# The attention's own values along the rows: four transposes of a broadcast column in place of a product of 512 columns

## The chip, the core and the metric

The kernel runs on one core of a Trainium2 chip. The metric is device time in microseconds (us) of one execution, the median of three runs. Five engines work side by side, each through its own instructions in order: PE (matrix products and transposes, its weight loads shown apart as PEld), DVE (elementwise work and reductions), ACT (activations and copies), POOL (here it issues the gathers) and SP (which issues most plain DMAs).

## The reference, cut to what matters

Sixty-four graphs of 256 nodes with 256 features pass through four layers over one adjacency matrix: two gated layers, an attention layer, a gated layer. The change touches the attention layer alone:

```
feats = jnp.einsum('bni,oi->bno', data, W1)
f1 = jnp.einsum('bno,o->bn', feats, W2) + b2[0]
logits = f1[:, :, None] + f1[:, None, :]
coefs = jax.nn.softmax(jax.nn.leaky_relu(logits) + bias1, axis=-1)
vals = jnp.einsum('bij,bjo->bio', coefs, feats)
return vals + bias2 + data
```

So each node has one number f1, its "own value". The logit of the pair (i, j) is f1 of i plus f1 of j. With nodes i on partitions and j along the row, f1 of i is a column (one number for each partition), and f1 of j has to be laid along the row of every partition. How this row is made is what changes. `bias1` is the adjacency matrix `adj`.

## The kernel before, in words

**Tiling.** Graphs go in pairs. A pair is `st["h"]` (nodes on partitions) and `st["hT"]` (features on partitions, `[128, 2, 2, 256]`: feature half, graph, node). Two streams, side a and side b, take turns over the pairs, so there are 16 rounds with two pairs each and 32 calls of `attention` (L430) in all. Everything is float32.

**Heavy and light work.** `beside` (L904) lays two things next to each other: the edge scores of one side's gated layer (`scores`, L695: tiles `ga` made on PE from `pre` and `pick`, in three PSUM buffers, and tiles `fetched` gathered by POOL's DMAs, both reduced by DVE to `junk` with a sum) and, as light work, what the other side does between its scores (`finish`, the two `turn`s, `attention`, and `before`, which makes the tables of the next layer). A `yield` of the light work says how many tiles of the heavy work are written out at that place; `yield 0` says none. Side a's attention stands beside side b's second gated layer, side b's attention beside side a's last one. At the end of a `beside`, `rm` is made from the scores and `spread` multiplies it on PE.

**Order.** The text of the program gives the order in which instructions are considered. The framework then lays down every engine's order before the run, from its own estimate of times, and lets an instruction that it takes to be ready go ahead of one that it takes to be waiting: the trace has the first `qb` product (L438) starting at 1667.54 us, in the midst of the transposes of `turn`, which are written ahead of it. At run time every engine keeps that order.

**PSUM.** `psum()` hands out one of five buffers, each one bank of 2 KB for each partition; `ga` has three more.

**The fetch.** `before` (L642) makes `pu` and `pv`, writes them to tables in DRAM (DMAs `tableu`, `tablev` from SP's queue), and POOL gathers from them (`fetch`, L807), each gather queued behind the one before it. The last gather of a layer has to land before DVE can finish that layer's scores, and `rm` after them.

**The attention, step by step.** At set-up, L257 makes `w2q`: the weights W1 transposed, with the product of W1 and W2 as column 256. `qb` (L255, L268) is that column repeated 128 times. Then, for each pair:

1. `rows` (L436) gets a product with `qb` as the stationary operand and all 512 columns of the pair, in two steps over the feature halves: every partition then holds f1 of all nodes along the row, without b2.
2. For each graph g and node half m, a product with `w2q` (257 columns) gives `feats` and, in column 256, f1 of the nodes on the partitions. DVE adds twice b2 to that column and puts it into `own` (L445, shown as `own_f` in the profile). ACT copies the 257 columns to `f`.
3. After both halves of a graph, ACT makes `logits` as `rows` plus `own` as its bias, two instructions for each graph.
4. DVE makes `e` from `logits` (leaky ReLU), adds `adj` with a running extreme `top`, and ACT takes the exponential into `e`. PE transposes `e`, and the products with `f` follow.

Of the kernel before, what the change touches and what calls it, by code (L numbers as in the profile page):

```python
# [9 lines left out]
FP = mybir.dt.float32  # L10
I32 = mybir.dt.int32
AF = mybir.ActivationFunctionType
ALU = mybir.AluOpType
AX = mybir.AxisListType

P = 128
B, N, D = 64, 256, 256
# [45 lines left out]
def blk(c):  # L63
    return slice(c * P, (c + 1) * P)
# [37 lines left out]
def adj_seq_kernel(ctx: ExitStack, tc: tile.TileContext, a: dict, out: bass.AP):  # L102
# [15 lines left out]
    tensor, vector, scalar = Noting(nc.tensor), Noting(nc.vector), Noting(nc.scalar)  # L118
    mm = tensor.matmul
# [6 lines left out]
    const = ctx.enter_context(tc.tile_pool(name="const", bufs=1))  # L126
# [3 lines left out]
    ident = const.tile([P, P], FP, name="ident")  # L130
# [13 lines left out]
    def vec(name, c):  # L144
        return vecs[:, VEC[name], c : c + 1]

    def sca(name):
        return scas[:, SCA[name] : SCA[name] + 1]
# [26 lines left out]
    for l in GNN:  # L175
        halfb2[l] = const.tile([P, 1], FP, name=l + "halfb2")
        vector.tensor_scalar(halfb2[l], sca(l + "b2"), 0.5, None, ALU.mult)
    twob2 = const.tile([P, 1], FP, name="twob2")
    vector.tensor_scalar(twob2, sca("L2_gnn_b2"), 2.0, None, ALU.mult)
    ones = const.tile([P, P], FP, name="ones")  # L180
    nc.gpsimd.memset(ones, 1.0)

# [69 lines left out]
    zbrow = const.tile([P, D], FP, name="zbrow")  # L252
    bias2 = const.tile([P, D], FP, name="bias2")
    w2q = const.tile([P, 2, D + 1], FP, name="w2q")
    qb = const.tile([P, 2, P], FP, name="qb")  # L255

    def attention_weights(one, psum):  # L257
        nc.scalar.dma_start(out=bias2, in_=a["L2_gnn_bias2"].partition_broadcast(P))
        nc.sync.dma_start(out=w2q[:, :, 0:D], in_=a["L2_gnn_W1T"].rearrange("(c p) e -> p c e", p=P))
        w2n = one.tile([P, 2, D], FP, tag="aT", name="w2n")  # L260
        nc.sync.dma_start(out=w2n, in_=a["L2_gnn_W1"].rearrange("(c p) e -> p c e", p=P))
        t = psum().rearrange("p a b -> p (a b)")
        for m in range(2):
            for c in range(2):
                mm(out=t[:, m : m + 1], lhsT=w2n[:, c, blk(m)], rhs=vec("L2_gnn_W2", c), start=c == 0, stop=c == 1)
        vector.tensor_copy(w2q[:, :, D], t[:, 0:2])
        for c in range(2):
            vector.tensor_scalar(qb[:, c, :], ones, w2q[:, c, D : D + 1], None, ALU.mult)  # L268

    def last_bias(one):  # L270
        bmrow = one.tile([P, D], FP, tag="hb", name="bmrow")
# [5 lines left out]
    def other_weights(one, psum):  # L277
        for l in GNN:
            z_weights(l)
            if l != GNN[0]:  # L280
                pre_weights(l)
            if l == GNN[1]:
                attention_weights(one, psum)
        last_bias(one)
# [10 lines left out]
    def stages(pools):  # L295
        fm, wk, one, ps, ga = (pools[k] for k in ("fm", "wk", "one", "ps", "ga"))
# [6 lines left out]
        def psum():  # L303
            return ps.tile([P, 2, 256], FP, tag="ps", name="ps")
# [7 lines left out]
        def flip(o, src):  # L312

            for m in range(2):
                for c in range(2):
                    tensor.transpose(o[:, m, blk(c)], src[:, c, blk(m)], ident)

        def hT_tile(st):
            return one.tile([P, 2, 2, N], FP, tag="hT" + st["side"], name="hT")

        def h_tile(st, g):
            return fm.tile([P, 2, D], FP, tag=f"h{g}" + st["side"], name=f"h{g}")
# [107 lines left out]
        def attention(st):  # L430
            hT, f = st["hT"], feats
            e, eT = [], []
            hb = st["h"]
            logits = one.tile([P, 2, 2, N], FP, tag="mT" + st["side"], name="logits")
            own = one.tile([P, 2, 2], FP, tag="own_f", name="own_f")
            rows = psum()  # L436
            for c in range(2):
                mm(out=rows, lhsT=qb[:, c, :], rhs=hT[:, c], start=c == 0, stop=c == 1)  # L438
            for g in range(2):
                e.append(one.tile([P, 2, N], FP, tag=f"e{g}", name=f"e{g}"))  # L440
                for m in range(2):
                    t = psum().rearrange("p a b -> p (a b)")
                    for c in range(2):
                        mm(out=t[:, 0 : D + 1], lhsT=hT[:, c, g, blk(m)], rhs=w2q[:, c, :], start=c == 0, stop=c == 1)
                    vector.tensor_scalar(own[:, g, m : m + 1], t[:, D : D + 1], twob2, None, ALU.add)  # L445
                    scalar.copy(f[g][:, m, 0 : D + 1], t[:, 0 : D + 1])
                    yield 0
                for m in range(2):
                    scalar.activation(
                        logits[:, g, m, :], rows[:, g, :], AF.Identity, bias=own[:, g, m : m + 1]  # L450
                    )
            for g in range(2):

                top = one.tile([P, 2], FP, tag=f"top{g}", name="top")
                vector.scalar_tensor_tensor(e[g], logits[:, g], 0.01, logits[:, g], ALU.mult, ALU.max)
                for m in range(2):
                    vector.tensor_tensor_reduce(
                        out=logits[:, g, m, :], in0=e[g][:, m, :], in1=adj[:, m, :], scale=-1.0, scalar=3.0e38,
                        op0=ALU.add, op1=ALU.min, accum_out=top[:, m : m + 1],
                    )  # L460
                for m in range(2):
                    scalar.activation(
                        e[g][:, m, :], logits[:, g, m, :], AF.Exp, bias=top[:, m : m + 1], scale=-1.0
                    )
                yield 2 - g
            st["h"], st["hT"] = [], hT_tile(st)

            def flip_h(g):
                t = psum()
                flip(t, st["h"][g])  # L470
                scalar.copy(st["hT"][:, :, g, :], t)


            st["flip"] = flip_h
            for g in range(2):
                t = psum()
                flip(t, e[g])
                eT.append(logits[:, g])
                scalar.copy(eT[g], t)
                yield 1  # L480
                h = h_tile(st, g)
                for m in range(2):
                    t = psum().rearrange("p a b -> p (a b)")
                    for c in range(2):
                        mm(out=t[:, 0 : D + 2], lhsT=eT[g][:, c, blk(m)], rhs=f[g][:, c, :], start=c == 0, stop=c == 1)
                    r = one.tile([P, 1], FP, tag="r", name="r")
                    vector.reciprocal(r, t[:, D + 1 : D + 2])
                    vector.scalar_tensor_tensor(h[:, m, :], t[:, 0:D], r, hb[g][:, m, :], ALU.mult, ALU.add)
                    if (g, m) == (1, 0):
                        flip_h(0)  # L490
                    yield 0, 1
                st["h"].append(h)

        return dict(psum=psum, product=product, load=load, mixed=mixed, finish=finish, attention=attention)


# [544 lines left out]
```

## Time and profile before

| what | value |
|---|---|
| median of three runs | 3490.05 us (3488.29 to 3501.34) |
| the profiled execution, its own time | 3499.89 us |
| its span, first to last instruction | 3498.2 us |
| mean granted TensorE clock | 0.993 |
| PE's idle time in all (span less busy) | 107 us |
| `ps<-hT,qb`, the products that are replaced | 128 records, median 592 ns |
| `ps<-w2q,hT` | 512 records, median 379 ns |
| `own_f`, DVE, 128x1 | 128, median 218 ns |
| `f<-ps`, ACT, 128x257 | 128, median 374 ns |
| `logits<-ps,own_f`, ACT, 128x256 | 128, median 479 ns |

How to read it: a float32 product appears as two records for each step over the features (64 products of 512 columns, 128 records), a transpose as one. PE's records overlap, since a product is still running out when the next begins; what a product takes of PE's time is read from the distance between starts, and not from its own length. In a timeline a row is a run of like instructions: its start, its length, the engine, the tiles (out<-in), the shape, how many, and in brackets how long the engine was idle before it and what ended that.

### The profile page before, as it was taken

The numbers are of one execution on the slowest core, as the hardware profiler recorded it, in microseconds if no ns is written. First come the engines' busy times: TensorE is split into PE (matmuls) and PEld (weight loads), VectorE is DVE, ScalarE is ACT, GpSimd is POOL, SyncE is SP. The second block draws the span as 40 slices with busy tenths as digits, with TensorE's granted clock in tenths as the row PEclk, the third lists the DMA queues.
The fourth block names the chain that finished last, engine by engine and source line by source line (L and its number), as shares of the span: only waits on it lengthen the run. The fifth ranks groups of instructions, "written<-read, shape, count | busy, mean of one in ns | idle before, by whom it ended". The sixth has DMA issues, their size and how long they took to land.

```text
span 3498.2 us, 48226 instructions
## 1 busy us (share of the span) xinstructions
PE 3391.1 (97%) x14200; PEld 2079.5 (59%) x14200; DVE 2626.2 (75%) x10526; ACT 1554.0 (44%) x2833; POOL 2409.6 (69%) x1882
## 2 busy tenths in 40 slices
PE   6999999999999999999999999999999999999998
PEld 3566565665656556565665656556565565656655
DVE  5777777777777777777777777777777777777776
ACT  2444444444444444544444444444444444444442
POOL 3767767677776767677677776776767667676765
PEclk7999999999999999999999999999999999999999
DMA  5788787877878878788787878778788788787875
GB/s 146 164 181 187 166 204 163 188 174 172 199 168 193 179 169 191 172 191 176 174 192 165 197 168 184 178 167 198 165 190 176 173 191 171 190 178 175 190 166 125
DMA packets 289070, 620.81 MB, mean 177 GB/s; under 512 B 39072, under 2 KB 56352, under 8 KB 288800
## 3 DMA queue, kind: packets, MB, share of 16 engines
q0 software_dynamic: 204800, 461.49, 66.6%
q1 hardware_dynamic: 82416, 154.96, 12.6%
q8 instruction: 115, 1.88, 0.2%
q10 hardware_dynamic: 1584, 1.20, 0.1%
q14 instruction: 155, 1.27, 0.1%
HBM read 500.06 MB, written 117.44 MB: 177 GB/s over the span
## 4 chain that ended last, share of the span: by engine, by line
PE 62%; POOL 10%; DMA 10%; DVE 8%; issue 7%; ACT 3%; another core or an unknown queue 0%; POOLq 0%; ACTq 0%; SPq 0%; DVEq 0%
PE ps L79 48%; PE ga L79 13%; POOL fetched L820 9%; DMA fetched<-tablev,ids_v 6%; DVE junk L79 3%; DMA fetched<-tableu,ids_u 3%; ACT pre L79 2%; DVE rm L79 1%; POOL left L820 1%; DVE sa L79 1%; DMA tableu<-pu 1%; DVE own L79 1%; ACT val L79 1%; ACT pu L79 1%; DVE mT L79 0%
## 5 line engine op out<-in xcount | busy, mean ns | idle before, releaser
L820 POOL DMA_INDIRECT fetched<-tablev,ids_v x832 | 1313.7, 1579 | 415.3 <-issue 256.1
L820 POOL DMA_INDIRECT fetched<-tableu,ids_u x832 | 840.5, 1010 | 548.8 <-DMA tableu<-pu 285.4
L79 DVE SCALAR_TENSOR_TENSOR junk<-fetched,L_gnn_w2row 128x256 f32<-128x256 f32 x1664 | 642.4, 418 | 205.8 <-DMA fetched<-tablev,ids_v 203.7
L79 PE MATMUL ga<-pre,pick 128*128 128x512 f32 x1408 | 721.5, 607 | 36.0 <-ACT pre L79 24.6
L79 PE MATMUL ps<-L_gnn_w,hT 128*128 128x512 f32 x1536 | 706.7, 597 | 5.8 <-DMA hT<-in_xT_dram 5.8
L79 DVE SCALAR_TENSOR_TENSOR junk<-ga,L_gnn_w2row 128x256 f32<-128x256 f32 x1408 | 537.3, 419 | 110.6 <-PE ga L79 94.6
L79 PEld LDWEIGHTS ps<-L_gnn_w,hT 128*128 128x128 f32 x1536 | 279.7, 190 | 323.2 <-issue 296.3
L79 ACT COPY pre<-pv 64x512 f32<-64x512 f32 x704 | 434.1, 617 | 70.8 <-DVE pv L79 47.3
L79 ACT COPY pre<-pu 64x1024 f32<-64x1024 f32 x352 | 361.4, 1044 | 7.4
L79 PE MATMUL ps<-sa,h 128*128 128x256 f32 x1536 | 359.8, 380 | 4.7 <-DVE sa L79 4.7
L79 PEld LDWEIGHTS ps<-sa,h 128*128 128x128 f32 x1536 | 291.7, 190 | 114.4 <-issue 62.5
L79 PEld LDWEIGHTS ga<-pre,pick 128*128 128x128 f32 x1408 | 248.5, 190 | 183.6 <-issue 92.5
L79 ACT COPY pu<-ps 128x256 f32<-128x256 f32 x384 | 142.8, 372 | 478.2 <-PE ps L79 450.3
L79 ACT ACTIVATE hb<-hT,L_gnn_zbias,scas 128x512 f32<-128x512 f32 x128 | 97.4, 807 | 479.3 <-DVE hT L79 368.1
L79 DVE TENSOR_TENSOR rm<-gva,val 128x256 f32<-128x256 f32 x768 | 279.8, 419 | 28.7 <-ACT val L79 21.2
L79 PE MATMUL ps<-adj,h 128*128 128x256 f32 x1280 | 296.8, 383 | 3.9 <-issue 3.9
L79 PEld LDWEIGHTS ps<-adj,h 128*128 128x128 f32 x1280 | 241.6, 191 | 74.1 <-issue 40.0
L79 DVE TENSOR_TENSOR pv<-ps,L_gnn_b1row 128x256 f32<-128x256 f32 x384 | 161.3, 420 | 135.5 <-ACT pu L79 128.8
L79 PEld LDWEIGHTS ps<-rm,gu 128*64 128x64 f32 x3072 | 174.7, 137 | 144.5 <-issue 54.1
L79 PE MATMUL ps<-rm,gu 128*64 128x128 f32 x3072 | 218.8, 280 | 32.6 <-DVE rm L79 31.0
L79 ACT COPY aT<-ps 128x512 f32<-128x512 f32 x192 | 112.4, 585 | 299.7 <-PE ps L79 267.5
L79 PE MATMUL ps<-mT,L_gnn_Wm 128*128 128x512 f32 x512 | 240.6, 592 | 0.0
(153 smaller groups left out, 4239.6 us busy)
## 6 DMA issues: line engine op xcount, KB each, us to landing
tableu<-pu SPq DMA_DIRECT2D x192, 256.0 KB
tablev<-pv SPq DMA_DIRECT2D x192, 256.0 KB
hT<-in_xT_dram SPq DMA_DIRECT2D x32, 512.0 KB
h<-in_x_dram SPq DMA_DIRECT2D x64, 256.0 KB
out_dram<-h SPq DMA_DIRECT2D x64, 256.0 KB
fetched<-tableu,ids_u POOLq DMA_INDIRECT x832
fetched<-tablev,ids_v POOLq DMA_INDIRECT x832
L_gnn_w<-in_L_gnn_W_dram SPq DMA_DIRECT2D x6, 256.0 KB
```

The source lines that it names most:

```text
L79: self.last = getattr(self.engine, op)(*a, **k)
L820: this = nc.gpsimd.indirect_dma_start(out=to, out_offset=None, in_=rows, in_offset=bass.IndirectOffsetOnAxis(ap=ids, axis=0), compute_op=( ...
```

## The change

The product with `qb` goes, and with it `qb`, `twob2` and `own`. In its place DVE takes column 256 of each `w2q` product, adds b2 and writes it 128 times side by side into the first 128 columns of `e[g][:, m]` (a tile that was there already, and is written anew later in the same call). A new inner function `across(g)` has PE transpose these two 128x128 squares into `rows[:, g]`, which lays f1 plus b2 along the row of every partition, and has ACT make the two `logits` of that graph with column 0 of the square as the bias. `across(0)` is called after the product of the second graph's first half (g, m) = (1, 0), and `across(1)` after the last product. So the logits of graph 0 are written down one product later than before, and PE's transposes read what DVE has written. Both terms now carry b2 once, where before one carried it twice.

```
-            own = one.tile([P, 2, 2], FP, tag="own_f", name="own_f")
             rows = psum()
-            for c in range(2):
-                mm(out=rows, lhsT=qb[:, c, :], rhs=hT[:, c], start=c == 0, stop=c == 1)
+
+            def across(g):
+
+                for m in range(2):
+                    tensor.transpose(rows[:, g, blk(m)], e[g][:, m, 0:P], ident)
+                for m in range(2):
+                    scalar.activation(
+                        logits[:, g, m, :], rows[:, g, :], AF.Identity, bias=e[g][:, m, 0:1]
+                    )
+
             for g in range(2):
                 e.append(one.tile([P, 2, N], FP, tag=f"e{g}", name=f"e{g}"))
                 for m in range(2):
                     t = psum().rearrange("p a b -> p (a b)")
                     for c in range(2):
                         mm(out=t[:, 0 : D + 1], lhsT=hT[:, c, g, blk(m)], rhs=w2q[:, c, :], start=c == 0, stop=c == 1)
-                    vector.tensor_scalar(own[:, g, m : m + 1], t[:, D : D + 1], twob2, None, ALU.add)
+
+                    vector.tensor_scalar(
+                        e[g][:, m, 0:P], t[:, D : D + 1].to_broadcast([P, P]), sca("L2_gnn_b2"), None, ALU.add
+                    )
                     scalar.copy(f[g][:, m, 0 : D + 1], t[:, 0 : D + 1])
                     yield 0
-                for m in range(2):
-                    scalar.activation(
-                        logits[:, g, m, :], rows[:, g, :], AF.Identity, bias=own[:, g, m : m + 1]
-                    )
+                    if (g, m) == (1, 0):
+                        across(0)
+            across(1)
```

At set-up these go as well:

```
-    twob2 = const.tile([P, 1], FP, name="twob2")
-    vector.tensor_scalar(twob2, sca("L2_gnn_b2"), 2.0, None, ALU.mult)
...
-    qb = const.tile([P, 2, P], FP, name="qb")
...
-        for c in range(2):
-            vector.tensor_scalar(qb[:, c, :], ones, w2q[:, c, D : D + 1], None, ALU.mult)
```

## The prediction

> **What bounds the kernel.** I read the page first, then PE's timeline around both kinds of attention, DVE's and ACT's there, and last the chain of waits.
>
> ```profile
> span 3498.2 us, 48226 instructions
> ...
> PE 3391.1 (97%) x14200; PEld 2079.5 (59%) x14200; DVE 2626.2 (75%) x10526; ACT 1554.0 (44%) x2833; POOL 2409.6 (69%) x1882
> ...
> PE 62%; POOL 10%; DMA 10%; DVE 8%; issue 7%; ACT 3%; another core or an unknown queue 0%; POOLq 0%; ACTq 0%; SPq 0%; DVEq 0%
> ```
>
> PE is idle for 107 us only, yet it holds 62% of the chain that ended last: POOL and the gathers' DMAs hold another 20%. Two things run neck and neck, PE's work and the path table, gather, landing, scores, `rm`. What is taken from PE counts where the chain lies on PE.
>
> PE around side b's attention (start, length, then what):
>
> ```profile
> 1709.56 1.07 PE L79 MATMUL ps<-ident,hT 128*128 128x128 f32 x8
> 1710.47 1.88 PE L79 MATMUL ps<-hT,qb 128*128 128x512 f32 x4
> 1712.19 3.64 PE L79 MATMUL ps<-w2q,hT 128*128 128x257 f32 x16
> 1715.66 1.89 PE L79 MATMUL ga<-adj,h 128*128 128x256 f32 x8
> 1717.39 1.02 PE L79 MATMUL ga<-pre,pick 128*128 128x512 f32 x2
> 1718.25 0.60 PE L79 MATMUL ps<-ident,e 128*128 128x128 f32 x4
> ```
>
> No brackets: PE starts each row as the last one lets it. The starts give prices: 1712.19 - 1710.47 = 1.72 us for the product with `qb`; 0.91 us for eight transposes, 0.11 us each; 3.47 us for the four `w2q` products, 0.87 us each. Between them and the transposes of `e` lie two rows of heavy work (1.73 and 0.86 us) that cover the softmax. All 32 calls show these distances: the transposes of `e` begin 6.06 us after the first `w2q` product every time.
>
> DVE and ACT on side a:
>
> ```profile
> 1670.99 0.22 DVE L79 TENSOR_SCALAR own_f<-ps,twob 128x1 f32<-128x1 f32 x1 [0.77 <-PE ps L79]
> 1671.86 0.22 DVE L79 TENSOR_SCALAR own_f<-ps,twob 128x1 f32<-128x1 f32 x1 [0.65 <-PE ps L79]
> ```
>
> ```profile
> 1671.24 0.37 ACT L79 COPY f<-ps 128x257 f32<-128x257 f32 x1 [1.47 <-DVE own_f L79]
> 1671.51 0.48 ACT L79 ACTIVATE logits<-ps,own_f 128x256 f32<-128x256 f32 x1
> 1672.11 0.37 ACT L79 COPY f<-ps 128x257 f32<-128x257 f32 x1
> ```
>
> DVE stands idle for the column and takes it 0.20 us after the product's end. ACT's copy of the same bank starts 0.03 us after DVE's read ends, though neither writes it: accesses of two engines to one bank come one after the other.
>
> **The change part by part.** *PE.* Each call loses 1.72 us and gains four transposes, 4 x 0.11 = 0.43 us (the row of four `ident,e`: 1718.68 - 1718.25 = 0.43 too). Net 1.29 us, 32 calls: 41.3 us of PE work. Their weight loads overlap, as in the rows of transposes that are there.
>
> *DVE.* 128 instructions become 128x128 from a column in PSUM. The trace has no such form. Bounds: `own_f` itself, 218 ns below; the slower of the two `qb<-ones,w2q` (128x128, 557 ns) above. Nearest is this row, of that size and from PSUM:
>
> ```profile
> L79 DVE TENSOR_TENSOR picko<-ps,scratch x2: 280/286/291, 47.9 to 48.1; 128x128 f32<-128x128 f32 x2
> ```
>
> I take 286 ns: 68 ns more, x128 = 9 us of DVE in all (0 to 43). On side a the idle 0.65 to 0.77 us before each `own_f` covers it; without that it costs 68 ns of delay each.
>
> *ACT, SP, POOL.* The same copies and logits; no DMA is added or moved. The set-up loses `twob2` and both `qb`, 0.98 us of DVE in the first 73 us, while other weights load; I count nothing (0 to 1 us gain).
>
> *The new waits.* PE's transposes now wait for DVE; behind them in PE's queue stand the heavy rows. On side a, taking the `qb` time out, `w2q` would start at 1669.92 - 1.72 = 1668.20. DVE is in `h<-ps,bias` until 1670.22, so the first two squares are done at 1670.79 (two times 286 ns); PE finishes the third product at 1668.20 + 2.60 = 1670.80: no stall. `across(1)` needs the fourth square (product done 1671.89, +0.20, +0.29 = 1672.38) and, by the one-after-the-other of a bank, the end of ACT's two reads for graph 0 (from about 1671.2, two times 0.48, so 1672.2). PE is free at 1671.89: 0.5 us, which the 1.73 us of `ga<-adj,h` fills if it is laid ahead.
>
> The Trainium skill's page "PSUM — Partial Sum Buffer" (PSUM bank collisions) says that any two engines on one bank and quadrant must be kept apart, reads too, which speaks against keeping both graphs in one bank as `rows` does; the 0.03 us above agrees, and the sum has that wait either way.
>
> *What is late next.* The transposes of `e`. Before, 2.77 us passed from the end of graph 0's second logits (1672.86) to the last exponential (1675.63). Now: 1672.2 + 2.77 = 1674.97, while PE gets there at 1668.20 + 3.47 + 0.43 + 1.73 + 0.86 = 1674.69. Late by 0.28 us. On side b DVE reaches the squares only behind `h<-ps,bias` (until 1712.69): two squares until 1713.27, transposes, logits to about 1714.7, exponentials to 1717.4, against PE at 1716.96: 0.5 us late, and up to 1.9 if three `hb` of 0.48 us stay ahead of the squares. The heavy row behind the transposes of `e` (0.86 us, in both timelines) can fill such a gap if it is laid ahead; it may or may not be, so I take half: 0.14 us for a, 0.25 for b.
>
> *What of it reaches the end.* I asked for the chain from 2 us before to 16 us after the first `w2q` product of each of the 32 calls. It lies on PE for over half of the stretch in 22 (15 of side a, 7 of side b), and on POOL, DMA and issue in 10 (1 and 9). One of the latter, side b at 1712, ends so:
>
> ```profile
> 1725.45 7.25 DMA fetched<-tablev,ids_v
> ...
> 1732.72 0.78 DVE junk L79 x4
> 1733.50 0.35 DVE pv L79
> ...
> 1737.86 1.12 PE ga L79 x2
> ```
>
> A gather lands, DVE does its scores and only then `pv`, which ACT and PE wait for. PE that comes 1.29 us sooner waits longer there: I count 0 for these ten (0 to 12.9 us). A gather that starts after an earlier gain starts sooner with it, so the 22 keep theirs: 22 x 1.29 = 28.4 us. Less 15 x 0.14 + 7 x 0.25 = 3.9. **Sum: -24.5 us**, from the profiled 3499.9 to 3475. The profiled execution is 9.8 us above the median; from the median it is 3465.5, say **3465**. Bounds of the parts: all 32 gain, nothing late, is -41.3 (3449); the 22 alone, a late by 0.28 and b by 1.9, is 28.4 - 4.2 - 13.3 = -11 (3479).
>
> **The rivals.** *The gathers take the whole over.* With 1.29 us less on PE in each call, more stretches become like 1712, and those that were PE's gain little. For: 20% of the chain is there, and PE waits for `rm` 33 times, 31.0 us. Against: after side a's attention the second half of `spread` starts 1.0 us after its `rm`, after side b's 1.9 us, so that the gain mostly fits in. If a third of it is left, -41.3 / 3 = -14: 3476; if none, 3490.
>
> *Slower: PE stands behind DVE.* Place: `across`, where a square is laid on DVE behind scores whose gather hasn't landed. The trace has DVE waiting for landings 148 times, 203.7 us, 1.4 us each. If both `across` of a call meet one, PE loses 2.8 us and gains 1.29: 32 x 1.5 = +48, 3538. It decides from 1.29 us of stall for each call. For: before, PE needed nothing of DVE for `rows`; now DVE's queue is PE's. Against: in none of the 32 calls were the transposes of `e` moved from their 6.06 us, so no landing got into this stretch.
>
> *The order falls out otherwise.* Engines are laid out anew from changed times over the whole kernel; waits that PE has now, such as 24.6 us for `ACT pre`, may grow or go. Either sign, about half a per cent: 3473 to 3507, taken as no change.
>
> *The clock.* The granted clock is 1.00 in the 2 us around the eight transposes at 1709.56. If transposes lowered it to half for the 3.47 us of `w2q` in each call, that would be 32 x 3.47 = 111 us more: 3576. The Trainium skill's "TensorE: Matmul & The Clock Gate" (Part 4: PE-mode transpose) says that transposes don't count as PE being busy for that clock; the trace, which has runs of eight at 1.00, bears out none of it.
>
> **How the numbers follow.** The forecast has 0.58; the gathers 0.16 (half of it past 0.5% faster); order 0.15; slower 0.09; the clock 0.02. Half a per cent, 17.5 us, is what a measurement of this kernel tells from no change. Faster (below 3472.6): most of the forecast's share, 0.52, half the gathers', 0.08, and 0.04 of the order's: 0.64. Slower (over 3507.5): 0.09 + 0.02 + 0.03 = 0.14. Same: 0.22. The range goes from all 32 gains with some 6 us of the runs' own spread, 3443, to where the slower case begins, 3502.
>
> **What would show it.** `ps<-hT,qb` is gone, 128 more records of transposes with `e` (0.11 us between starts); the new DVE form near 286 ns; the transposes of `e` begin 6.5 us after the first `w2q` product, not 6.06, without a bracket of over 0.5 us; PE's busy time down by 30 to 45 us. Wrong it is if PE's waits for `e` or `ACT logits` sum to over 20 us, if the squares stand behind scores on DVE, or if PE's idle time (107 us) grows by what its work lost.

## The result, and the profile after

The changed kernel takes 3468.32 us (median of 7 runs, 3455.23 to 3472.99) against 3490.05 us. The medians lie 22 us apart. The ratio over all 14 runs (their means are 3465.75 and 3492.72 us) is 0.9923 with a 95% interval of 0.9903 to 0.9943: 27 us faster, 20 to 34. It was forecast at 3465. From here on, 27 us is the gain that the experiments have to account for.

The page of the changed kernel: span, busy time of each engine, the chain by engine.

```profile
span 3466.6 us, 48384 instructions
...
PE 3361.7 (97%) x14200; PEld 2067.6 (60%) x14200; DVE 2639.6 (76%) x10523; ACT 1557.2 (45%) x2833; POOL 2416.1 (70%) x1882
...
PE 68%; POOL 9%; DMA 7%; issue 7%; DVE 6%; ACT 3%; ACTq 0%; POOLq 0%; DVEq 0%
```

PE's busy time fell by 29 us, just short of the 30 to 45 that the prediction named as a sign; its idle time stayed (107 us before, 105 now), and its share of the chain rose from 62 to 68%.

PE around side b's attention:

```profile
1693.57 1.07 PE L79 MATMUL ps<-ident,hT 128*128 128x128 f32 x8
1694.48 2.77 PE L79 MATMUL ps<-w2q,hT 128*128 128x257 f32 x12
1697.09 0.27 PE L79 MATMUL ps<-ident,e 128*128 128x128 f32 x1
1697.20 0.60 PE L79 MATMUL ps<-w2q,hT 128*128 128x257 f32 x2
1697.63 0.27 PE L79 MATMUL ps<-ident,e 128*128 128x128 f32 x1
1697.74 0.60 PE L79 MATMUL ps<-w2q,hT 128*128 128x257 f32 x2
1698.18 1.03 PE L79 MATMUL ga<-adj,h 128*128 128x256 f32 x4
1699.04 0.38 PE L79 MATMUL ps<-ident,e 128*128 128x128 f32 x2
1699.26 1.03 PE L79 MATMUL ga<-adj,h 128*128 128x256 f32 x4
1700.13 1.02 PE L79 MATMUL ga<-pre,pick 128*128 128x512 f32 x2
1700.99 0.81 PE L79 MATMUL ps<-ident,e 128*128 128x128 f32 x4
```

Again no brackets: the four new transposes were laid between products that PE had to do anyway, graph 1's in the midst of `ga<-adj,h`, and PE waits for none of them. From `ident,hT` to the transposes of the exponentials (the last row) it is 7.42 us, where it was 8.69. That last row takes 0.81 us, where it took 0.60: behind the first of the four, the weight load for the others waits for an exponential, which has come late.

```profile
1701.25 0.31 PEld L79 LDWEIGHTS ps<-ident,e 128*128 128x128 f32 x3 [0.26 <-ACT e L79]
```

DVE's new form (least, median and most ns):

```profile
L79 DVE TENSOR_SCALAR e<-ps,scas x128: 334/344/352, 177.3 to 3393.5; 128x128 f32<-128x128 f32 x128
```

Where the gain is and where part of it stays is best read in stretches of PE's row. I took the starts of four kinds of rows in every round and the mean over the rounds: from `ident,hT` to the first transposes of the exponentials; from there to the first product of `before`; on to `spread`; and on to the next attention's `ident,hT`.

| stretch, us | a before | a after | b before | b after |
|---|---|---|---|---|
| turn to exponentials | 8.65 | 7.50 | 8.68 | 7.41 |
| to `before` | 6.94 | 6.80 | 6.80 | 7.01 |
| to `spread` | 10.46 | 10.46 | 13.87 | 13.67 |
| to the next turn | 16.34 | 17.09 | 141.58 | 141.54 |
| all | 42.40 | 41.85 | 170.95 | 169.64 |

In the first two rows, which hold the attention, a gains 1.29 us and b 1.06 (1.27 less the 0.21 of the late exponential): 16 x 2.35 = 38 us. Side a gives 0.75 back in the row "to the next turn". There PE waits for `ACT pre`: 1.0 us in each round before, now up to 2.3. One such place, in the chain of waits of the changed kernel (start, length, what; pieces of `issue` left out):

```profile
398.42 1.55 POOL fetched L824
...
400.28 7.62 DMA fetched<-tablev,ids_v
...
407.92 0.78 DVE junk L79 x4
408.70 0.35 DVE pv L79
...
413.05 1.13 PE ga L79 x2
```

It is the picture that the prediction showed for side b: the last gather lands, DVE does its scores, then `pv`, then ACT's `pre`, and PE's product waits for that.

Of the 12 us that side a gives back in 16 rounds, 8.6 are longer waits. In the rest PE's rows themselves run slower, as here, behind a wait:

```profile
1677.79 2.08 PE L79 MATMUL ga<-pre,pick 128*128 128x512 f32 x2 [2.25 <-ACT pre L79]
1679.80 1.71 PE L79 MATMUL ps<-rm,gu 128*64 128x128 f32 x16
```

In the kernel before, these rows take 1.12 and 1.09 us. The granted clock is 0.50 from 1677.68 to 1681.09 us. Leaving out the first 120 us and the last 40 us, the changed kernel has three such stretches of 3.4 us, each behind a wait of PE of 1.9 to 2.4 us (two for `ACT pre`, one ahead of `ps<-sa,h`); the kernel before has none. Not every wait of that length brings one: behind the 2.33 us at 410.72 the clock stays at 1.00. Half the speed for 10.2 us is 5 us, a part of the difference between the 38 us of the table and the 29 us by which PE's busy time fell.

### The profile page after: what moved, and what is told of

Same layout as the page of the kernel before. It is cut to its first block, busy times and chain, and to the rows that moved or that the text cites. A ratio compares the mean times of both kernels' runs of the same rounds, so it can differ in the third digit from the quotient of the medians.

```text
span 3466.6 us, 48384 instructions
## 1 busy us (share of the span) xinstructions
PE 3361.7 (97%) x14200; PEld 2067.6 (60%) x14200; DVE 2639.6 (76%) x10523; ACT 1557.2 (45%) x2833; POOL 2416.1 (70%) x1882
## 3 DMA queue, kind: packets, MB, share of 16 engines
q14 instruction: 155, 1.27, 0.1%
## 4 chain that ended last, share of the span: by engine, by line
PE 68%; POOL 9%; DMA 7%; issue 7%; DVE 6%; ACT 3%; ACTq 0%; POOLq 0%; DVEq 0%
PE ps L79 52%; PE ga L79 16%; POOL fetched L824 8%; DMA fetched<-tablev,ids_v 4%; DVE junk L79 3%; ACT pre L79 2%; DMA fetched<-tableu,ids_u 2%; DVE rm L79 1%; DMA tableu<-pu 1%; POOL left L824 1%; DVE sa L79 1%; ACT val L79 1%; ACT pu L79 1%; DVE own L79 0%; DVE pv L79 0%
## 5 line engine op out<-in xcount | busy, mean ns | idle before, releaser
L79 PE MATMUL ga<-pre,pick 128*128 128x512 f32 x1408 | 723.5, 609 | 37.0 <-ACT pre L79 27.4
L79 PE MATMUL ps<-rm,gu 128*64 128x128 f32 x3072 | 218.7, 281 | 23.0 <-DVE rm L79 22.6
L79 PE MATMUL ps<-aT,L_gnn_Wa 128*128 128x512 f32 x512 | 240.6, 592 | 0.0
```

The source lines that it names most:

```text
L79: self.last = getattr(self.engine, op)(*a, **k)
```

## The experiments

My theory: PE has 1.29 us less to do in each call, the heavy rows cover the new waits, and the gathers keep some of the gain from the end. Rivals: the gain comes from another order of the engines' instructions; DVE's wider writes count; the missing part is lost in the attention itself. Ratios are to the kernel before, run beside each on the same chip.

### DVE's part alone

```
-                    vector.tensor_scalar(own[:, g, m : m + 1], t[:, D : D + 1], twob2, None, ALU.add)
+                    vector.tensor_scalar(
+                        e[g][:, m, 0:P], t[:, D : D + 1].to_broadcast([P, P]), twob2, None, ALU.add
+                    )
...
-                        logits[:, g, m, :], rows[:, g, :], AF.Identity, bias=own[:, g, m : m + 1]
+                        logits[:, g, m, :], rows[:, g, :], AF.Identity, bias=e[g][:, m, 0:1]
```

> The kernel before, with its product of 512 columns kept, and only DVE's part of the change: the column is written 128 times into e instead of once into own. If the gain comes from PE's work (my theory), nothing of it is here: DVE has 128 x 126 ns = 16 us more (344 ns in the changed kernel against 218), which PE's work covers, so 3480 to 3500 us beside 3490 before. If DVE's work counts in full, 16 us slower, 3506. If the gain comes from another order of the engines' work, which the change of one DVE form can bring as well, some 3470.

Measured: 3562.11 us, ratio 1.0192 (1.0165 to 1.0218), 67 us slower. All three expectations missed it. PE's timeline around side a's attention in this kernel:

```profile
1047.69 1.02 PE L79 MATMUL ga<-pre,pick 128*128 128x512 f32 x2
1048.55 0.60 PE L79 MATMUL ps<-ident,e 128*128 128x128 f32 x4
1048.98 1.88 PE L79 MATMUL ga<-pre,pick 128*128 128x512 f32 x4
1050.70 1.91 PE L79 MATMUL ps<-f,logits 128*128 128x258 f32 x8
1052.45 0.60 PE L79 MATMUL ps<-ident,e 128*128 128x128 f32 x4
1053.78 1.14 PE L79 MATMUL ps<-f,logits 128*128 128x258 f32 x4 [0.73 <-ACT logits L79]
```

Three heavy products (`ga<-pre,pick`, 0.86 us, two records each) are there to cover the softmax. In the kernel before one stands ahead of each pair of transposes' products: one before the first `ident,e`, one behind it, one behind the second. Here two stand behind the first, none behind the second, and PE waits 0.73 us for ACT's copy (the last bracket). One DVE form was changed, and the order laid down ahead of the run put one product elsewhere, and with it rows of DVE and ACT.

These waits sum to 22.9 us. The greater part of the 67 us stands later: side a's stretch "to the next turn" takes 19.25 us, where it took 16.34, which is 47 us in 16 rounds. There PE waits for `ACT pre` (53.3 us in this run, 24.6 before), and the granted clock falls to 0.50 in twelve stretches, 44 us together, each behind a wait of 2.2 to 3.1 us: up to 22 us of the loss.

### Both calls of across at the end

```
-                    if (g, m) == (1, 0):
-                        across(0)
+            across(0)
             across(1)
```

> The changed kernel with both calls of across after the last product. Graph 0's logits are written down one product (0.87 us) later. If the heavy rows cover the softmax, as they did before, PE does the same work in about the same time: 3468 us within 6. If the place of across(0) carries the gain, by starting the softmax of graph 0 early, PE waits for e up to 0.87 us in each call, 28 us: up to 3496.

Measured: 3494.81 us, ratio 0.9996 (0.9982 to 1.001). The whole gain is gone, though PE does the same work. Its timeline on side a:

```profile
1032.23 1.88 PE L79 MATMUL ga<-pre,pick 128*128 128x512 f32 x4
1033.94 0.60 PE L79 MATMUL ps<-ident,e 128*128 128x128 f32 x4
1034.38 1.02 PE L79 MATMUL ga<-pre,pick 128*128 128x512 f32 x2
1035.28 2.01 PE L79 MATMUL ps<-f,logits 128*128 128x258 f32 x8
1037.12 0.60 PE L79 MATMUL ps<-ident,e 128*128 128x128 f32 x4
1038.45 1.14 PE L79 MATMUL ps<-f,logits 128*128 128x258 f32 x4 [0.73 <-ACT logits L79]
```

It waits not for the first exponentials, as I had written, but at the same place as the last kernel in the attention: here two heavy products went ahead of the first transposes, and again none was left behind the second. These are PE's longest waits in this kernel, summed (us in total, times, longest):

```profile
PE ga L79 <- ACT pre L79: 44.5, 32, 2.4
PE ps L79 <- ACT logits L79: 22.6, 31, 0.7
```

The first of the two lines has grown as well (24.6 us in the kernel before, 27.4 in the changed one): side b's stretch "to `spread`" now takes 15.08 us (13.67 in the changed kernel).

### The heavy products held in their place

Both kernels again, with a heavy product of the attention's stretch held behind the transposes that it is written after: `behind` asks that an instruction be issued after the one written last before it on the same engine. (`held` is emptied when `attention` ends.)

```
+            held.append(True)
             for g in range(2):
                 t = psum()
                 flip(t, e[g])
...
-                    with stay(tensor):
+                    with behind(tensor) if held else stay(tensor):
                         mm(out=t, lhsT=pick[:, k, 4 * m + i, :], rhs=pre[:, n], start=True, stop=True)
```

> Both across after the last product, as in the run before (3495 us), and the heavy products of the attention's stretch held behind the transposes of e that they are written after. In that run one of three heavy products (0.86 us) had gone ahead of the first transposes of e, and none was left to cover ACT's copy between the second transposes and their products: PE waited 0.73 us for ACT logits in each call, 22.6 us in all. If that one product's place is the cause, this kernel is back at the changed kernel's time, 3466 to 3478 us (ratio 0.992 to 0.995), with no such wait and at most 0.9 us of wait for e in its stead. If the later logits are the cause, it stays at 3490 to 3500.

Measured: 3468.7 us, ratio 0.9934 (0.9919 to 0.9948). The wait for `ACT logits` is gone and the gain is back with `across(0)` still at the end, so that its place is not what carries the gain. Between the traces of these two kernels 29 us have gone: 9 in the stretches from `ident,hT` to `before`, where the product was put back, and 20 in side b's stretch "to `spread`" (13.80 us again), where PE waits for `ACT pre` (20.4 us in all, in place of 44.5). The hold has laid out DVE's and ACT's rows anew as well, so that the product's place alone isn't shown to make those 20 us.

> The kernel before with DVE's squares alone (3562 us in the run before, 1.9% slower), and the same hold on the heavy products, which gives PE the order of the kernel before in that stretch. If the one product's place makes the 67 us, this kernel is at 3490 to 3505 (ratio 0.998 to 1.003), since DVE's 16 us are covered. If DVE's work or the later copies of f and logits behind it make them, it stays over 3540.

Measured: 3514.81 us, ratio 1.0061 (1.0043 to 1.008). PE's order is now that of the kernel before, row for row, and 46 of the 67 us are gone; 21 stay, more than I expected. Of the 46, 36 came back in side a's stretch "to the next turn" (16.97 us, in place of 19.25); DVE's and ACT's orders were laid out anew here too, so that again PE's order alone isn't shown to bring them. One wait for `ACT logits` is left, now behind the first transposes of the exponentials:

```profile
PE ps L79 <- ACT logits L79: 12.6, 24, 0.6
```

The stretch from the exponentials' transposes to `before` is 7.47 us on side a and 7.44 on side b (6.94 and 6.80 in the kernel before): 1.17 us in a round, 19 us in 16. So in the old order DVE's wider writes, or what is laid out otherwise on DVE and ACT because of them, do cost; in the changed kernel's order they don't. DVE's and ACT's orders differ from those before in this run, so that the two can't be told apart here.

### PE's work given back, and taken further

The product put back into `rows` ahead of the transposes:

```
             rows = psum()
+            for c in range(2):
+                mm(out=rows, lhsT=w2q[:, c, 0:P], rhs=hT[:, c], start=c == 0, stop=c == 1)
```

> The changed kernel with a product of 512 columns put back in front of the transposes; its result is overwritten by them. PE gets its 1.72 us for each call back, 32 x 1.72 = 55 us more than the changed kernel and 14 us more than before. If PE's work sets the end for about two thirds of what is taken from it (27 of 41 us, as measured), it gives 3468 + 0.65 x 55 = 3504 us, 9 to 14 us over before. If the gain came from the other order or from logits that start later, the time stays at 3460 to 3475.

Measured: 3510.36 us, ratio 1.0042 (1.0028 to 1.0056): 14.7 us over the kernel before, where PE's work is 13.8 us over it. With the changed kernel's text and the product back, the gain is gone. (DVE's and ACT's orders are not quite those of the changed kernel.)

Neither product nor transposes; f1 along the row is left out, and `adj` stands in its place:

```
-                for m in range(2):
-                    tensor.transpose(rows[:, g, blk(m)], e[g][:, m, 0:P], ident)
...
-                        logits[:, g, m, :], rows[:, g, :], AF.Identity, bias=e[g][:, m, 0:1]
+                        logits[:, g, m, :], adj[:, m, :], AF.Identity, bias=e[g][:, m, 0:1]
```

> The changed kernel with neither the product nor the transposes: f1 along the row is left out, the logits take adj in its place. PE has 4 x 0.11 x 32 = 14 us less than the changed kernel. If two thirds of PE's work go on reaching the end: 9 us less than the changed kernel, 3459 us. If the gathers have taken over by now, no less than 3466.

Measured: 3454.79 us, ratio 0.9891 (0.9868 to 0.9913): 38 us under the kernel before, 11 more than the change, of 14 us less PE work. Set against the kernel before, PE's work of 14 us more, 41 less and 55 less gave 15 us more, 27 less and 38 less.

### The gathers taken back

All gathers of v rows left out, in the kernel before and in the changed one:

```
             for f, x in now:
+                if x == 1:
+                    continue
                 rows = st["tables"][x]
```

> The kernel before without the gathers of the v rows (half of all gathers; the scores are those of the u rows alone), so that the path over POOL and the gathers is short. It is the base for the next run. PE then sets the end nearly everywhere: its busy time of 3391 us less what waits are in it, some 3370 to 3440 us.

> The changed kernel without the gathers of the v rows, beside the run before it. If the gathers hold back what PE gains, as in 10 of 32 calls by my count, the difference of these two is the whole of PE's gain, 32 x 1.29 = 41 us at most (by the timelines of the changed kernel 16 x 1.16 + 16 x 1.27 = 39), and not the 25 us that the full kernels differ by. If something in the attention itself holds it back, DVE or ACT, the difference stays at 22 to 28 us.

Measured: 3757.35 us, ratio 1.077 (1.0734 to 1.0806), and 3732.0 us, 1.0685 (1.0656 to 1.0714). With half of the gathers gone both are over 6% slower, against every expectation, and 0.85 points apart with an uncertainty of 0.46: that tells 39 us from 25 no better than a guess. The orders of PE, DVE and ACT are the same as with the gathers. PE's longest wait in the first of the two is new:

```profile
PE ps L79 <- DVE sa L79: 111.5, 48, 5.7
```

DVE's `sa` waits in its turn for something that the profile can't name. Of the 259 us by which this trace is longer than that of the kernel before, 163 are idle time of PE and 95 longer busy time. The clock has a part in the latter: it was granted at 0.50 for 167 us, in 38 stretches. I don't know why fewer gathers bring these waits, and the pair decides nothing.

Fewer gathers left out, the v gathers of the last tiles alone:

```
+                if x == 1 and f in (7, 8, 9):
+                    continue
```

> The changed kernel without the v gathers of the tiles 7, 8 and 9, the last ones of each layer's path (those scores are then of the u rows alone). PE, DVE and ACT keep the changed kernel's order, instruction for instruction; POOL's path is one to three gathers of 1.9 us shorter. In the changed kernel eight of side a's sixteen stretches wait for a gather's landing after the attention (PE waits up to 2.3 us for ACT pre in place of 1.0). If the gathers hold back the missing part of PE's gain, that wait is at its 1.0 us in all sixteen, and this kernel is 6 to 20 us faster than the changed one: 0.987 to 0.990 of before. If the missing part has another cause, it is at 0.992 again.

> The kernel before with the same gathers left out, orders again as in the kernel before. The difference between this one and the run above is then PE's gain without the gathers: by the timelines 16 x (1.29 + 1.06) = 38 us if my theory holds, where the full kernels differ by 27. If the gathers are not the cause, the two differ by 25 to 29 us again.

Measured: 3443.37 us, ratio 0.9836 (0.9809 to 0.9864), and 3482.27 us, ratio 0.9939 (0.9921 to 0.9958). Their medians differ by 38.9 us and their ratios by 36 us, where 38 was the sum by the timelines and the full kernels differ by 27 by their ratio. By the intervals alone (1.03 points, give or take 0.33, against 0.77 give or take 0.20) the two differences are not apart; the traces show the place. The chain, and PE's wait for `pre`, in the changed kernel with the tail out:

```profile
PE 90%; DVE 4%; ACT 3%; issue 2%; DMA 1%; POOL 0%; another core or an unknown queue 0%; ACTq 0%; POOLq 0%; DVEq 0%
```

```profile
PE ga L79 <- ACT pre L79: 17.6, 20, 1.0
```

POOL has left the chain, and no wait for `ACT pre` is longer than 1.0 us (2.3 in the changed kernel), and outside the first 120 and the last 40 us the clock is granted in full in both runs. A round's side a, which gained 0.55 us with all gathers (the table above), gains 1.23 (42.52 to 41.29), side b 1.23 (169.61 to 168.38): together 2.46 us, 39 in 16 rounds. So, by these two traces, the gathers held back what was missing: by the waits that end with them, and by the lower clock behind such waits.

### A bank for each graph's row

```
-            rows = psum()
 
             def across(g):
 
+                rows = psum()
                 for m in range(2):
-                    tensor.transpose(rows[:, g, blk(m)], e[g][:, m, 0:P], ident)
+                    tensor.transpose(rows[:, 0, blk(m)], e[g][:, m, 0:P], ident)
...
-                        logits[:, g, m, :], rows[:, g, :], AF.Identity, bias=e[g][:, m, 0:1]
+                        logits[:, g, m, :], rows[:, 0, :], AF.Identity, bias=e[g][:, m, 0:1]
```

> The changed kernel with a PSUM bank of its own for each graph's row, so that the transposes of graph 1 needn't wait for ACT's reads of graph 0's row. If heavy rows cover that wait, as I counted, the time is that of the changed kernel within 0.3%: 0.990 to 0.995 of before. If the wait in one bank costs what it can (0.5 us in each call), 16 us faster: 0.988. If a sixth buffer among five makes PE wait for a free bank, slower: 0.996 or more.

Measured: 3477.68 us beside 3501.7, ratio 0.9934 (0.9913 to 0.9955), as the changed kernel. The shared bank costs nothing that can be measured here.

### Eight gathers ahead

An attempt at a better kernel, from what the kernel without the tail showed:

```
-FETCHES = [(0, 0), (1, 0), (2, 0), (0, 1), (3, 0), (1, 1)]
-FETCHES += [(-1, 0), (2, 1), (4, 0), (3, 1), (-1, 1), (5, 0), (6, 0), (4, 1), (7, 0), (5, 1), (6, 1), (7, 1)]
+FETCHES = [(0, 0), (1, 0), (2, 0), (0, 1), (3, 0), (1, 1), (2, 1), (3, 1)]
+FETCHES += [(-1, 0), (4, 0), (-1, 1), (5, 0), (6, 0), (4, 1), (7, 0), (5, 1), (6, 1), (7, 1)]
...
-AHEAD = 6
+AHEAD = 8
```

> The changed kernel with eight gathers in place of six issued after the first half of a layer's tables; two v gathers that read that half only are drawn forward in the list, nothing is left out. If POOL's queue has room there, the last gather of each layer lands up to 3 us sooner, the waits that the run without the tail took away go, and this is 6 to 25 us faster than the changed kernel: 0.985 to 0.990 of before. If POOL is held by the order of its queue anyway, or the draw comes while the other side's gathers are due, it stays at 0.992 or is slower.

Measured: 3637.09 us, ratio 1.0425 (1.0399 to 1.045). PE, DVE and ACT keep their order; only POOL's queue differs. Among its longest waits:

```profile
POOL left L824 <- DMA left<-tableu,left_u: 238.1, 95, 5.6
```

With two v gathers drawn forward, the v gather of `left` came to stand two places behind its own u gather, which has to land first, and POOL's whole queue stood for 2.5 us in each layer (238.1 over 95). PE's waits for `rm` rose to 100.0 us. So the place of a gather in the list matters, and no kernel here that leaves nothing out beats the changed one.

## Why the prediction was right, point by point

**PE's work.** Forecast: 1.29 us less in each call. Measured to the exponentials: 1.15 us on side a, 1.27 on side b; with the next row, 1.29 and 1.06. The transposes of `e` begin 6.50 us after the first `w2q` product on side b, as forecast, and 7.28 us on side a, where six of the transposes of `turn` were laid behind that product's start. The run with the product put back lost all of the gain, so PE's work is the cause.

**DVE's form** was mis-sized: 286 ns taken, 344 measured, 126 ns over `own_f` and not 68, inside the bounds. That it is covered holds in the changed kernel, where PE waits for no square. It doesn't hold in general: with the squares alone and PE's order as before (DVE's and ACT's were not), 21 us were lost.

**The new waits.** Forecast: no stall at `across(0)`, 0.5 us at `across(1)` that `ga<-adj,h` fills. So it came, down to the row that fills it. The bank of its own confirmed that the wait in one bank is covered.

**The exponentials being late.** Forecast: 0.28 us on side a and 0.5 on side b, half of it felt, 3.9 us in all. On side a it cost nothing. On side b no bracket stands in PE's row, but the row of four transposes is 0.21 us longer, as its weight load shows, and so is the stretch "to `before`" (7.01 us, in place of 6.80): 3.4 us in 16 calls, about what was forecast, though on one side alone.

**The step that failed: "The heavy row behind the transposes of `e` (0.86 us, in both timelines) can fill such a gap if it is laid ahead".** I took that as a gain. It was the greatest risk of this change: the transposes of the exponentials were hardly late, and the two kernels in which such a row was laid elsewhere were slower than their held versions by 22 us (both calls at the end: 0.62 points between the ratios) and 46 (the squares alone: 1.31 points). How much of this is the row's own place, and how much DVE's and ACT's other orders, stays open; its own trace is the wait for `ACT logits`, 22.6 and 22.9 us. The forecast had "the order falls out otherwise" as no change, within half a per cent; one order tried here was 1.9% slower. The changed kernel kept the rows' places, which the forecast couldn't know: that was luck.

**The gathers.** Forecast: 22 calls keep their gain, 10 don't, of these 9 on side b. The sum was good; the sides were not. In the changed kernel's chain the stretch lies on POOL, DMA and issue for over half in 11 calls, 8 of them on side a, so that the waits are on the other side now. By its own terms the forecast had 17 us on side a and 7 on side b; by the table it was 9 and 21. That the sum came out was luck in part. That these waits are what is missing, the traces of the runs with the tail out showed (39 us by their rounds, where 38 of PE's gain can be counted); the times alone don't tell it. What the forecast didn't have is the clock behind the longer waits, some 5 us of the 11.

**The other rivals.** DVE's queue in front of PE never came about: no square stood behind a landing. The clock was granted at 0.993 before and 0.991 after, and the three stretches at 0.50 come behind waits. What the Trainium skill's page "TensorE: Matmul & The Clock Gate" (Part 4: PE-mode transpose) says of transposes and the clock is not seen here: in the changed kernel none of these stretches begins behind a row of transposes.

## What to carry to other kernels

When the engine that sets the end is full, count what an edit takes off it between starts, and then look for the next path that runs beside it: here more than a quarter of the gain (11 of 38 us) stayed with the gathers and with the lower clock behind PE's longer waits. The work that covers a wait is a stock with places; when an edit changes an estimate that the order is laid from, look in the new order where each covering row went, before looking at any duration, and hold the rows by an explicit dependence if their places matter. With one product of 0.86 us in another place, and DVE's and ACT's rows laid out anew with it, nearly all that the change gained was lost.

## What the runs showed of the hardware

In these traces a wait of PE of 1.9 to 3.1 us can be followed by 3.4 us (once 6.8 us) at a granted clock of 0.50, so that the wait costs more than its own length: three times in the changed kernel, twelve times with the squares alone, and never in the kernel before (all outside the first 120 and the last 40 us); a row of two `ga` products behind it took 2.08 us, in place of 1.12. A DVE instruction that adds a scalar to a column of PSUM, read 128 times, took 344 ns, where a two-input form of the same size from PSUM took 286. Leaving out half of the gathers, in unchanged orders, made the kernel 7.7% slower, with waits that the profile can't name and a granted clock of 0.973; the cause is open.
